# Four graph layers on TensorE: two more dense products in seven-product form, three norms' sums on ScalarE, and a plan with refined times

## The chip, the cores and the metric

The kernel runs on one core of a Trainium2 chip. The metric is the device time of one execution in microseconds (us). The core's engines are called by their short names: PE is TensorE (matmul), DVE is VectorE, ACT is ScalarE, POOL is GpSimd, SP is SyncE, which here only issues transfers.

## What is computed

A batch of 32 samples, each with 512 tokens of 256 features (x) and an own 512 x 512 weighted adjacency, goes through four layers in float32. Every layer adds its result to its input and normalizes each token over its 256 features:

```
x = layernorm(x + L0(x))   # agg = adj@x + (1+eps)*x;  relu(agg@W1 + b1) @ W2 + b2      256 -> 512 -> 256
x = layernorm(x + L1(x))   # h = adj @ (x@W.T + b);  where(h > 0, h, alpha*h)          256 -> 256
x = layernorm(x + L2(x))   # h = layernorm(x);  x + relu((adj@h)@W_rel + b_rel + h@W_root)
x = layernorm(x + L3(x))   # agg = adj@x + eps*x;  silu(rmsnorm(agg@W1 + b1)) @ W2 + b2 256 -> 1024 -> 256
```

`layernorm(v)` is `(v - mean) / sqrt(var + 1e-5)`, with mean and variance over the features of a token.

## The kernel before, in words

**Layout.** The 512 tokens lie on 128 partitions in four chunks (NC = 4), so x of one sample is a tile of 128 x 4 x 256, one "room" of SBUF. There are 38 rooms of 4 KB a partition, 12 small tiles ("few") of 64 numbers, and eight PSUM banks ("ps").

**Seven products.** A product of two 2 x 2 block matrices can be had from seven block products and some sums of blocks instead of eight block products (`seven`, line 554). The sums of the left factor come from `left_sums` (572) and, for weights, once for the whole run, from `weight_sums` (588); those of the right factor from `right_sums` (580), four subtractions per use. `seven` hands over each product as it is done: `take` and `put` add it from PSUM to the result, or copy it there. Three PSUM banks hold the running products. Before the change this form is used for the aggregation with the adjacency (`aggregate`, 649), for the first dense layers of layers 0 and 3 (`dense_feat`, 689) and for the second dense layer of layer 3 (written out inside `layer3`, lines 891 to 931, with 128-column matmuls).

**Eight products.** The second dense layer of layer 0, the dense layer of layer 1 and the two dense layers of layer 2 (W_root and W_rel, added up in one PSUM bank) use `dense_tok` (677). It takes one half of the tokens (two chunks) at a time and runs matmuls with 256 moving columns: four chunks of the contraction times two token chunks per half in layers 0 and 2.

**Norms.** `Norm` (740) is used by all four layers. `half` takes the statistics of two chunks on DVE, with `bn_stats` (128x256 to six numbers) and `bn_aggr` (to mean and variance). `scales` turns variances into `1/sqrt` with a POOL power. `scaled` applies scale and shift to each chunk, on ACT or DVE. Layer 1 takes two scalings from the same statistics, for its own norm and for the one that opens layer 2.

**The order.** Nothing is issued in program order. Every operation is first recorded in a `Plan` (178) with a cost for each engine that may run it (lines 35 to 68). `order` (303) then lists the operations: it keeps a clock per engine, picks the engine that can start first, and on it, among operations that could start within SOON, the one with the lowest rank. The rank is the sample's number times a period of 50 us plus the moment at which TensorE will need the result (`needs`, 273). Up to four samples are under way at a time (FLIGHT). Rooms, small tiles and banks are handed out in that order, with some kept back from later samples. YIELD makes an operation that could run on ACT or DVE prefer ACT. `best` (297) tries the RULES and keeps the order that its own clock likes most. What comes out is fixed in advance: each engine's queue runs strictly in that order, with semaphores between engines. All operations are issued from two places, so the profile shows them under line 248 (the order's `issue`) and tells them apart by tiles and shapes.

Of the kernel before, what the change touches and what calls it, by code (L numbers as in the profile page):

```python
# [2 lines left out]

# [10 lines left out]
P = 128  # L14
# [5 lines left out]
def span(ap):  # L20

    n = 1
    for d in ap.shape[1:]:
        n *= d
    return n
# [19 lines left out]


def stats_time(n):
    return 0.095 + n * 0.00092, 0.082


def scalar_time(n):
    return 0.19 + n * 0.00078, 0.1

# [19 lines left out]

SOON = 0.1


YIELD = 0.4

# [3 lines left out]

RULES = [(50, 2, last, 2) for last in (12, 20)]

# [93 lines left out]
class Plan:  # L178
# [52 lines left out]

    def do(self, out, *ways, ordered=None):

        ins = []
        port = set()
        for e, method, _, args, kw in ways:
            tiles = [x for x in (*args, *kw.values()) if isinstance(x, (bass.AP, Part))]
            ins += tiles
            if e == "gpsimd" and kw.get("op") != ALU.pow or e == "vector" and not (
                method.startswith("bn_") or any(in_psum(x) for x in tiles)  # L240
            ):
                port.add(e)

        def issue(engine, method, args, kw):
            def put(x):
                return x.place() if isinstance(x, Part) else x

            getattr(getattr(self.nc, engine), method)(  # L248
                put(out), *(put(x) for x in args), **{k: put(x) for k, x in kw.items()}
            )  # L250

        self.add(
            {
                e: (times, lambda e=e, m=method, args=args, kw=kw: issue(e, m, args, kw))
                for e, method, times, args, kw in ways
            },
            out, ins, ordered, port,
        )
# [127 lines left out]
def tile_gnn_stack(ctx: ExitStack, tc: tile.TileContext, a: dict, out: bass.AP):  # L386
# [35 lines left out]
    FH = FC3 // 2  # L422
    FLIGHT, ROOMS, SMALL = 4, 38, 12

# [21 lines left out]

    def scalar(func, n, x, **kw):
        return "scalar", "activation", scalar_time(n), (x,), dict(func=func, **kw)

# [8 lines left out]
    def act(o, x, func, **kw):  # L458
        plan.do(o, scalar(func, span(o), x, **kw))

    def copy(o, x):
# [18 lines left out]
    def stt(o, x, s, y, op0, op1):  # L480
        plan.do(o, vector("scalar_tensor_tensor", span(o), x, s, y, op0=op0, op1=op1))

# [66 lines left out]
    make_identity(nc, ident)  # L549
    mhalf = constant("mhalf", [P, 2 * NC])  # L550
    nc.vector.memset(mhalf, -0.5)

# [26 lines left out]

    def right_sums(b11, b12, b21, b22, t):  # L580

        sub(t[0], b12, b11)
        sub(t[1], b22, t[0])
        sub(t[2], b22, b12)
        sub(t[3], b21, t[1])
        return dict(m1=b11, m2=b21, m3=b22, m4=t[3], m5=t[0], m6=t[1], m7=t[2])

# [7 lines left out]
    def quarters(W):  # L595

        n = W.shape[-1] // 2
        return (W[:, k, i * n : (i + 1) * n] for i in range(2) for k in range(2))


    class Adjacency:
# [33 lines left out]
        def with_loops(self, loop):  # L635
            for d, o in zip(self.plain, self.loops):
                add(o, d, loop.unsqueeze(1).to_broadcast(list(o.shape)))

# [10 lines left out]
    def aggregate(x, adjacency):  # L649
# [5 lines left out]
        t = room(4, HC, P)  # L655
        right = right_sums(*blocks, [t[:, i] for i in range(4)])

# [31 lines left out]
    def dense_feat(aT, left, bias, hT, done):  # L689


        n = hT.n // 2
        t = room(4, TH)
        right = right_sums(
            *(aT[:, k, j * TH : (j + 1) * TH] for k in range(2) for j in range(2)),
            [t[:, i, :] for i in range(4)],
        )
        for f0 in range(0, n, 2):
# [22 lines left out]
            seven(*(bank(2, TH) for _ in range(3)), product, take, put)  # L721

    def column_sums(t, put):

# [15 lines left out]
    class Norm:  # L740


        def __init__(self, r):
            self.r = r
            few = small(64)
            cut = lambda at, n: few[:, at : at + n]
            self.st = [cut(6 * c, 6) for c in range(NC)]
            self.mv = cut(24, 2 * NC).then(lambda v: v.rearrange("p (c i) -> p c i", i=2))
            self.ve, self.rstd, self.shift = (cut(32 + 8 * i, 8) for i in range(3))

        def half(self, h):
            for c in range(h * HC, (h + 1) * HC):
                r = self.r[:, c, :]
                plan.do(self.st[c], ("vector", "bn_stats", stats_time(D), (r,), {}))
                plan.do(self.mv[:, c, :], ("vector", "bn_aggr", stats_time(6), (self.st[c],), {}))

        def scales(self, *affine):

            n = self.n = len(affine) * NC
            for i, (m, plus) in enumerate(affine):  # L760
                o = self.ve[:, i * NC : (i + 1) * NC]
                ts(o, self.mv[:, :, 1], m, plus, ALU.mult, ALU.add)
            inv_sqrt(self.rstd[:, 0:n], self.ve[:, 0:n])

        def scaled(self, i=0):

            y = self.r if (i + 1) * NC == self.n else tok()
            s, shift = (t[:, i * NC : (i + 1) * NC] for t in (self.rstd, self.shift))
            stt(shift, self.mv[:, :, 0], -1.0, s, ALU.mult, ALU.mult)
            for c in range(NC):  # L770
# [3 lines left out]
                    vector(  # L774
                        "tensor_scalar", D, r, self.mv[:, c, 0:1], scale,
                        op0=ALU.subtract, op1=ALU.mult,
                    ),
                    scalar(AF.Identity, D, r, scale=scale, bias=shift[:, c : c + 1]),
                )
            return y  # L780

    def plus_row(x, r):
# [21 lines left out]
    def layer0(x, adjacency):  # L804
# [7 lines left out]
        norm = Norm(x)  # L812
        for h in range(2):
            ps = dense_tok([(h1.chunk(k), W2_0[:, k, :]) for k in range(FC0)], h)
            add(half(x, h), ps, half(x, h))
            norm.half(h)
        norm.scales((1.0, LN_EPS))
# [28 lines left out]
    def layer2(h, xx, u, adjacency):  # L846
# [8 lines left out]
        norm = Norm(xx)  # L855
        for h in range(2):
            ps = dense_tok(
                [(hT.chunk(k), Wroot[:, k, :]) for k in range(DC)]
                + [(aT[:, k, :], Wrel[:, k, :]) for k in range(DC)], h,
            )  # L860
            add(half(u, h), ps, half(u, h))
            stt(half(xx, h), half(u, h), 0.0, half(xx, h), ALU.max, ALU.add)
            norm.half(h)
        adjacency.with_loops(loop3)
        norm.scales((1.0, LN_EPS))
        return norm.scaled()

    def layer3(x, adjacency, b):
# [20 lines left out]
        for c in range(NC):  # L889
            flip(pr[:, c * P : (c + 1) * P], rstd[:, c : c + 1].spread(P, P))  # L890
        t1, t2, t4 = (room(FH, TH) for _ in range(3))
        for q in range(0, FH, 2):
            for f in (q, q + 1, FH + q, FH + q + 1):
                mul(hT.chunk(f), hT.chunk(f), pr)
                act(hT.chunk(f), hT.chunk(f), AF.Silu, scale=w_3[:, f : f + 1])
            b11, b12 = (hT.pair(q)[:, :, j * TH : (j + 1) * TH] for j in range(2))
            b22 = hT.pair(FH + q)[:, :, TH:N]
            t1q, t2q = t1[:, q : q + 2], t2[:, q : q + 2]
            sub(t1q, b12, b11)
            sub(t2q, b22, t1q)  # L900
            sub(b12, b22, b12)
            sub(t4[:, q : q + 2], hT.pair(FH + q)[:, :, 0:TH], t2q)
        norm = Norm(x)

        def block(i, j):
            return x[:, j * HC : (j + 1) * HC, i * P : (i + 1) * P]

        def factor(m, k):
            if m in ("m4", "m5", "m6"):
                return dict(m4=t4, m5=t1, m6=t2)[m][:, k, :]  # L910
            f = k if m in ("m1", "m7") else FH + k
            j = 0 if m in ("m1", "m2") else 1
            return hT.chunk(f)[:, j * TH : (j + 1) * TH]

        def product(m, ps, first):
            for k in range(FH):
                for i in range(HC):
                    mm(
                        ps[:, i, :], factor(m, k)[:, i * P : (i + 1) * P], A2_3[m][:, k, :],
                        first and i == 0 and k == 0, k == FH - 1,  # L920
                    )

        def take(ps, i, j):
            add(block(i, j), ps, block(i, j))

        def put(ps, i, j, more):
            take(ps, i, j)
            if i == 1:
                norm.half(j)

        seven(*(bank(HC, P) for _ in range(3)), product, take, put)
        norm.scales((1.0, LN_EPS))
# [15 lines left out]
    b2_0 = row("L0_gnn_b2")  # L948
    W2_0 = weight("L0_gnn_W2")
    alpha = row("L1_gnn_alpha")  # L950
    nalpha = constant("nalpha", [P, 1])
# [10 lines left out]
    shift_2 = fold_norm(Wroot, "shift_2")  # L962
    add(shift_2, shift_2, b_2)
    h = layer1(x, adjacency)
    W1_3 = weight("L3_gnn_W1")
# [7 lines left out]
    A1_3 = weight_sums("A1_3", *quarters(W1_3))  # L973
    A2_3 = weight_sums(
        "A2_3",
        *(W2_3[:, k * FH : (k + 1) * FH, i * P : (i + 1) * P] for i in range(2) for k in range(2)),
    )
    layer3(layer2(*h, adjacency), adjacency, 0)
# [46 lines left out]
```

## Time and profile before

| | us |
|---|---|
| median of three runs | 2394.66 (2393.58 to 2394.78) |
| the profiled execution's own time | 2392.34 |
| its span, first to last instruction | 2390.6 |
| PE busy | 2361.3 |
| PE weight loads busy | 2113.1 |
| DVE busy | 2076.0 |
| ACT busy | 1195.2 |
| POOL busy | 391.1 |

A row of the profile names line, engine, operation, tiles written and read, shape and count; then the busy time of the group, the mean duration of one in nanoseconds, the engine's idle time just before them, and what ended that idle time. Tile names stand without numbers: `A` are sums of weights, `L_gnn_W` weights, `room`, `few` and `ps` as above. A float32 matmul leaves two records, each with a weight load of its own; a transposition by the identity (`ident`) leaves one. Durations in a group overlap where an engine is pipelined, so the busy time (a union) divided by the count can be below the mean. In the slices, each digit is the busy share of a fortieth of the span in tenths.

The largest waits that the trace shows are of engines that have little to do: POOL waited 1558.3 us for small DVE results, ACT 735.6 us for PE. DVE waited 202.7 us for PE and 42.6 for ACT. PE waited 10.3 us for the first x, 6.9 for DVE and 2.6 for ACT.

### The profile page before, as it was taken

What the parts mean: (1) busy time and instruction counts of PE and PEld (TensorE: products, weight loads), DVE (VectorE), ACT (ScalarE), POOL (GpSimd) and SP (SyncE); (2) the same over time, 40 slices, a digit from 0 to 9 for tenths busy, and PEclk for the clock granted to TensorE, in tenths of its full rate; (3) what the DMA queues carried; (4) which work ended last, traced back from release to release, by engine and by line L of the source; (5) the groups of instructions that cost most, each with busy time, mean ns of one, the idle gap of its engine ahead of it and who ended that gap; (6) DMA issues with size and microseconds to landing.
All of it is one profiled execution on the core that took longest, in us unless ns stands there. A gap on an engine that the chain in (4) does not pass through costs nothing.

```text
span 2390.6 us, 36106 instructions
## 1 busy us (share of the span) xinstructions
PE 2361.3 (99%) x12808; PEld 2113.1 (88%) x12808; DVE 2076.0 (87%) x5449; ACT 1195.2 (50%) x2417; POOL 391.1 (16%) x422
## 2 busy tenths in 40 slices
PE   7999999999999999999999999999999999999998
PEld 6889889988889888898888989888898888988887
DVE  6978988889888898888988888988889888888798
ACT  2445555455544455544555445554445554444564
POOL 1111111111112111211111111111111111111111
PEclk9999999999999999999999999999999999999999
DMA  7001013011111011110111101111101111010100
GB/s 229 14 1 33 30 54 95 18 39 53 54 51 43 14 53 54 51 49 9 52 53 54 49 23 37 53 54 49 47 12 53 54 49 55 12 54 1 54 1 36
DMA packets 104548, 107.47 MB, mean 45 GB/s; under 512 B 10928, under 2 KB 79280, under 8 KB 104368
## 3 DMA queue, kind: packets, MB, share of 16 engines
q1 hardware_dynamic: 100208, 104.62, 14.1%
q8 instruction: 101, 1.65, 0.3%
q10 hardware_dynamic: 4160, 0.54, 0.2%
q14 instruction: 79, 0.65, 0.1%
HBM read 54.80 MB, written 16.78 MB: 30 GB/s over the span
## 4 chain that ended last, share of the span: by engine, by line
PE 95%; DVE 3%; DMA 1%; ACT 1%; issue 0%; POOLq 0%; POOL 0%; ACTq 0%; SPq 0%; DVEq 0%
PE ps L248 95%; DVE room L248 2%; DVE few L248 1%; ACT room L248 1%; DMA room<-room 0%; DMA room<-in_adj_dram 0%; DMA L_gnn_ln_gamma_c<-in_L_gnn_ln_gamma_dram 0%; DMA L_gnn_b_c<-in_L_gnn_b_dram 0%; ACT L248 0%; POOLq L1021 0%; POOL few L248 0%; DVE L_gnn_W L248 0%; DVE A L248 0%; SPq L264 0%; ACTq L1021 0%
## 5 line engine op out<-in xcount | busy, mean ns | idle before, releaser
L248 PE MATMUL ps<-room,room 128*128 128x256 f32 x3584 | 951.8, 381 | 14.0 <-DMA room<-in_x_dram 10.3
L248 PEld LDWEIGHTS ps<-room,room 128*128 128x128 f32 x3584 | 646.7, 191 | 94.2 <-DMA room<-in_x_dram 10.3
L248 DVE TENSOR_TENSOR room<-ps,room 128x256 f32<-128x256 f32 (+1 forms) x1024 | 531.0, 526 | 212.7 <-PE ps L248 166.9
L248 PE MATMUL ps<-L_gnn_W,room 128*128 128x128 f32 (+1 forms) x3584 | 667.1, 320 | 2.6 <-ACT room L248 1.5
L248 PEld LDWEIGHTS ps<-L_gnn_W,room 128*128 128x128 f32 x3584 | 581.6, 191 | 61.1 <-ACT room L248 2.4
L248 DVE TENSOR_TENSOR room<-room,room 128x512 f32<-128x512 f32 (+1 forms) x928 | 500.5, 557 | 10.2 <-DMA room<-in_adj_dram 4.6
L248 ACT ACTIVATE room<-room,few 128x256 f32<-128x256 f32 x588 | 311.6, 592 | 328.5 <-DVE few L248 328.4
L248 ACT ACTIVATE room<-ps 128x256 f32<-128x256 f32 (+1 forms) x545 | 220.3, 407 | 498.5 <-PE ps L248 494.6
L248 POOL TENSOR_TENSOR few<-few,mhalf 128x4 f32<-128x4 f32 (+1 forms) x160 | 200.4, 1253 | 1558.5 <-DVE few L248 1558.3
L248 ACT ACTIVATE room<-ps,L_gnn_b_c 128x256 f32<-128x256 f32 x768 | 320.1, 470 | 246.1 <-PE ps L248 241.0
L248 PE MATMUL ps<-room,L_gnn_W 128*128 128x256 f32 x1536 | 439.5, 379 | 2.9 <-DVE room L248 2.8
L248 PE MATMUL ps<-room,A 128*128 128x256 f32 x1152 | 323.9, 379 | 0.2 <-ACT room L248 0.2
L248 PEld LDWEIGHTS ps<-room,L_gnn_W 128*128 128x128 f32 x1536 | 285.0, 190 | 40.0 <-DVE room L248 4.7
L248 DVE TENSOR_TENSOR room<-room 128x256 f32<-128x256 f32 (+1 forms) x576 | 266.8, 478 | 16.4 <-DMA room<-in_adj_dram 10.8
L248 POOL TENSOR_TENSOR room<-room,L_gnn_b 128x256 f32<-128x256 f32 x256 | 190.8, 753 | 434.9 <-PE ps L248 261.6
L248 ACT ACTIVATE room<-room 128x1024 f32<-128x1024 f32 (+1 forms) x256 | 238.2, 947 | 31.9 <-DVE room L248 31.2
L248 PEld LDWEIGHTS ps<-A,room 128*128 128x128 f32 x1536 | 226.9, 191 | 16.5
L248 PEld LDWEIGHTS ps<-room,A 128*128 128x128 f32 x1152 | 210.2, 190 | 27.1 <-ACT room L248 0.6
L248 PE MATMUL ps<-A,room 128*128 128x128 f32 x1536 | 233.4, 274 | 0.0
L248 DVE BATCH_NORM_STATS2 few<-room 128x6 f32<-128x256 f32 x512 | 203.9, 405 | 0.3
L248 ACT ACTIVATE room<-room,L_gnn_rms_weight_c 128x512 f32<-128x512 f32 x256 | 167.5, 712 | 73.0 <-DVE room L248 72.8
L248 DVE TENSOR_TENSOR room<-room,ps 128x512 f32<-128x512 f32 x256 | 161.9, 681 | 2.6 <-PE ps L248 2.5
(44 smaller groups left out, 1263.8 us busy)
## 6 DMA issues: line engine op xcount, KB each, us to landing
room<-in_adj_dram SPq DMA_DIRECT2D x128, 256.0 KB, 4.8
room<-room SPq DMA_DIRECT2D x256, 128.0 KB, 2.2
room<-in_x_dram SPq DMA_DIRECT2D x32, 512.0 KB, 5.9
out_dram<-room SPq DMA_DIRECT2D x32, 512.0 KB, 3.0
L_gnn_W<-in_L_gnn_W_dram SPq DMA_DIRECT2D x2, 1024.0 KB, 7.6
L_gnn_W<-in_L_gnn_W_dram SPq DMA_DIRECT2D x2, 512.0 KB, 5.3
L_gnn_b<-in_L_gnn_b_dram ACTq DMA_DIRECT2D x3, 128.0 KB, 4.2
L_gnn_W_rel<-in_L_gnn_W_rel_dram SPq DMA_DIRECT2D x1, 256.0 KB, 5.2
```

The lines of the kernel that those rows point to most:

```text
L248: getattr(getattr(self.nc, engine), method)(put(out), *(put(x) for x in args), **{k: put(x) for k, x in kw.items()})
```

## The change

There are four parts.

1. **Two more places in seven products.** `dense_sums` and `dense_add` are made out of what stood in `layer3`, and layers 0 and 2 use them in place of `dense_tok`. In layer 2, the transposed h and the aggregate are the two halves of one contraction of 512, W_root and W_rel the two halves of its weights, so that its two dense layers become one. With layer 0's second dense layer these are the "three more dense layers" of the change. `dense_tok` stays in layer 1. Two more sets of weight sums, A2_0 and A_2, are made once.
2. **Mean and variance of three norms on ACT.** The norms of layers 0, 1 and 2 take, per chunk, an Identity activation whose sum over the row is kept (`accum_out`), a DVE multiplication of two chunks' sums by -1/256, and a Square activation with that as its bias whose sum is kept. The element-wise results are not read; they go to two places, `scrap0` and `scrap1`, in turn. The norm of layer 3 keeps `bn_stats` and `bn_aggr` (`NormOnVector`).
3. **Fewer rooms.** 36 instead of 38. `right_sums` writes one of its four results over a block of its input. Layer 3's sums lie in six half-filled rooms where they lay in three full ones, layers 0 and 2 take three half-filled ones each.
4. **The plan's figures.** ACT's cost now depends on how many of scale and bias are columns; summing activations and DVE operations with a column have costs of their own. SOON goes from 0.1 to 0.06, YIELD from 0.4 to 0.8, and six RULES are tried instead of two. `with_loops` is named as vector work, as it was.

```diff
+def columns_time(n):
+    return 0.12 + n * 0.00106, 0.085
-def scalar_time(n):
-    return 0.19 + n * 0.00078, 0.1
+def scalar_time(n, columns):
+    return 0.035 + n * 0.00089 + columns * 0.113, 0.105
+def total_time(n, columns):
+    return 0.187 + n * 0.00089 + columns * 0.1, 0.1
-SOON = 0.1
-YIELD = 0.4
-RULES = [(50, 2, last, 2) for last in (12, 20)]
+SOON = 0.06
+YIELD = 0.8
+RULES = [(50, 2, last, near) for last in (12, 20) for near in (0, 0.5, 1)]
...
-    FLIGHT, ROOMS, SMALL = 4, 38, 12
+    FLIGHT, ROOMS, SMALL = 4, 36, 12
...
+    def total(o, x, func, **kw):
+        plan.do(o, scalar(func, span(x), x, times=total_time, **kw), scrap=next(scraps))
...
+    scraps = cycle([constant(f"scrap{i}", [P, D]) for i in range(2)])
...
+    def dense_sums(upper, lower):
+        right = {}
+        for pairs in zip(upper, lower):
+            blocks = [x[:, :, j * TH : (j + 1) * TH] for x in pairs for j in range(2)]
+            sums = right_sums(*blocks, [room(2, TH) for _ in range(3)], blocks[1])
+            for m, x in sums.items():
+                right.setdefault(m, []).extend(x[:, e, :] for e in range(2))
+        return right
+
+    def dense_add(x, right, left, done):
+        def block(i, j):
+            return x[:, j * HC : (j + 1) * HC, i * P : (i + 1) * P]
+        def product(m, ps, first):
+            n = len(right[m])
+            for k in range(n):
+                for i in range(HC):
+                    mm(
+                        ps[:, i, :], right[m][k][:, i * P : (i + 1) * P], left[m][:, k, :],
+                        first and i == 0 and k == 0, k == n - 1,
+                    )
+        def take(ps, i, j):
+            add(block(i, j), ps, block(i, j))
+        def put(ps, i, j, more):
+            take(ps, i, j)
+            if i == 1:
+                done(j)
+        seven(*(bank(HC, P) for _ in range(3)), product, take, put)
...
         def half(self, h):
-            for c in range(h * HC, (h + 1) * HC):
-                r = self.r[:, c, :]
-                plan.do(self.st[c], ("vector", "bn_stats", stats_time(D), (r,), {}))
-                plan.do(self.mv[:, c, :], ("vector", "bn_aggr", stats_time(6), (self.st[c],), {}))
+            chunks = range(h * HC, (h + 1) * HC)
+            for c in chunks:
+                total(self.first[:, c : c + 1], self.r[:, c, :], AF.Identity)
+            mine = slice(h * HC, (h + 1) * HC)
+            ts(self.less[:, mine], self.first[:, mine], -1.0 / D, None, ALU.mult)
+            for c in chunks:
+                total(
+                    self.second[:, c : c + 1], self.r[:, c, :], AF.Square,
+                    bias=self.less[:, c : c + 1],
+                )
...
-        for h in range(2):
-            ps = dense_tok([(h1.chunk(k), W2_0[:, k, :]) for k in range(FC0)], h)
-            add(half(x, h), ps, half(x, h))
-            norm.half(h)
+        dense_add(x, dense_sums(h1.rooms[:1], h1.rooms[1:]), A2_0, norm.half)
...
-        for h in range(2):
-            ps = dense_tok(
-                [(hT.chunk(k), Wroot[:, k, :]) for k in range(DC)]
-                + [(aT[:, k, :], Wrel[:, k, :]) for k in range(DC)], h,
-            )
-            add(half(u, h), ps, half(u, h))
+        def done(h):
             stt(half(xx, h), half(u, h), 0.0, half(xx, h), ALU.max, ALU.add)
             norm.half(h)
+        dense_add(u, dense_sums(hT.rooms, [aT]), A_2, done)
...
-        norm = Norm(x)
+        norm = NormOnVector(x)
+        dense_add(x, right, A2_3, norm.half)
...
+    A2_0 = weight_sums("A2_0", *blocks_of(W2_0[:, 0:2], W2_0[:, 2:]))
+    A_2 = weight_sums("A_2", *blocks_of(Wroot, Wrel))
```

## The prediction

> **What bounds the kernel now.** I read the page's busy table and slices first, to see whether one engine is full throughout.
>
> ```profile
> PE 2361.3 (99%) x12808; PEld 2113.1 (88%) x12808; DVE 2076.0 (87%) x5449; ACT 1195.2 (50%) x2417; POOL 391.1 (16%) x422
> PE   7999999999999999999999999999999999999998
> DVE  6978988889888898888988888988889888888798
> PEclk9999999999999999999999999999999999999999
> ```
>
> PE (TensorE matmul) is busy in all slices but the first and last, at full granted clock. DVE is second, ACT half empty. A busy PE is not yet a binding one, so the chain of waits in order of time comes next: is PE's stretch broken anywhere?
>
> ```profile
> by line: PE ps L248 94.5%; DVE room L248 2.1%; DVE few L248 0.8%; ACT room L248 0.7%; DMA room<-room 0.4%; issue 0.4%; DMA room<-in_adj_dram 0.2%; DMA L_gnn_ln_gamma_c<-in_L_gnn_ln_gamma_dram 0.2%; DMA L_gnn_b_c<-in_L_gnn_b_dram 0.2%; ACT L
> ...
> 315.74 1818.33 PE ps L248 x9853
> ```
>
> 1818 us on end the chain never leaves PE: the middle is paced by matmul issue. Idle PE is 2390.6 - 2361.3 = 29.3 us, 17 of it before 150 us, 2 around 2130 to 2180 us and 11 at the very end. So the sum is: change of PE work, plus change of PE's idle time.
>
> Rows' mean durations overlap (matmuls are pipelined), so the pitch is read from PE's timeline, start to next start:
>
> ```profile
> 425.97 1.89 PE L248 MATMUL ps<-L_gnn_W_root,room 128*128 128x256 f32 x8
> 427.70 0.60 PE L248 MATMUL ps<-ident,few 128*128 128x128 f32 x4
> ...
> 430.73 2.17 PE L248 MATMUL ps<-L_gnn_W,room 128*128 128x128 f32 x18
> 432.73 0.60 PE L248 MATMUL ps<-L_gnn_W_rel,room 128*128 128x256 f32 x2
> ```
>
> A float32 matmul leaves two records. 256 columns: (427.70 - 425.97) / 4 = 0.432 us. 128 columns: (432.73 - 430.73) / 9 = 0.222 us; I take 0.224, since ten such records from 2347.86 us on take 1.12 us to the next start.
>
> **PE's part.** dense_tok of layers 0 and 2 goes: 16 matmuls of 256 columns each, times 32 samples, 1024. dense_add replaces it: 7 products x 2 chunks x 2 row blocks = 28 of 128 columns, 56 per sample, 1792. The layer-3 product had this form already and keeps its 56. Sum: 1792 x 0.224 - 1024 x 0.432 = 401.4 - 442.4 = -41.0 us.
>
> One rule of the Trainium skill speaks against this: "TensorE: Matmul & The Clock Gate", section "Back-to-back issue gap", says that in a stream of load-then-multiply pairs the spacing is set by both, about 81 ns at 128 columns and 131 ns at 512, so that halving the columns saves much less than half. Interpolated to 98 ns at 256 (my estimate from that page), the 128-column matmul would cost 0.83 of 0.432, 0.357 us, and the change would add 1792 x 0.357 - 442.4 = +197 us. The row decides: 0.222 us in a run of nine, each with its own weights loaded. A float32 pass is long enough to cover its load. I take -41.0.
>
> **DVE's part.** Its rows:
>
> ```profile
> L248 DVE TENSOR_TENSOR room<-ps,room 128x256 f32<-128x256 f32 x608 | 248.3, 419 | 176.5 <-PE ps L248 140.8 <-ACT room L248 32.1
> L248 DVE TENSOR_TENSOR room<-room,room 128x512 f32<-128x512 f32 x480 | 321.0, 685 | 6.1 <-DMA room<-in_adj_dram 4.6 <-ACT room L248 0.5
> L248 DVE BATCH_NORM_STATS2 few<-room 128x6 f32<-128x256 f32 x512 | 203.9, 405 | 0.3
> L248 DVE BATCH_NORM_AGGREGATE few<-few 128x2 f32<-128x6 f32 x512 | 86.6, 171 | 2.7
> ```
>
> Busy time over count is each price: 0.408, 0.669, 0.398, 0.169. Removed: 384 statistics (-152.8) and 384 aggregates (-64.9), three norms of four; 128 PSUM adds of 512 elements at 0.682 (-87.3). Added: 448 PSUM adds of 256 elements, seven per layer (+182.8); 256 right-hand sums of 512 elements, four per layer (+171.3); 256 two-column negations, nearest the four-column scalar row at 0.147 (+37.6); 160 shifts change form, -160 x 0.268 + 160 x 0.195 (-11.7). Chunks that the planner moves between ACT and DVE, from the two instruction queues: 35 fewer normalizations, 22 more copies (-4.6). Eight weight sums once (+3.2). In all +74 us, to 2150, or 67.2 us a sample, where PE needs 2320 / 32 = 72.5.
>
> In the middle all of it lies beside PE work. Cover for it: 9.8 us of DVE idleness per sample now (2390.6 - 2076.0 over 32), of which 2.3 are filled and 1.3 vanish with PE's own shortening. How full may DVE be before PE stalls? Busy time by stretch answers:
>
> ```profile
> 350.00:1000.00 650.00, 650.00 (x3547) 583.26 (x3546) 570.91 (x1500) 329.51 (x669) 110.25 (x118) 1.00 0.15 48
> ...
> 2300.00:2360.00 60.00, 60.00 (x416) 56.49 (x415) 55.48 (x122) 32.21 (x59) 7.26 (x7) 1.00 0.00 1
> ```
>
> Columns after the length are PE, PEld, DVE, ACT, POOL. DVE at 87.8% over 650 us and at 92.5% over 60 us cost PE nothing; the fullest 50 us stretch (850 to 900) has 47.8 us, 95.6%, PE still whole. The new mean, 2150 / 2357 = 91%, lies inside what short stretches show and above what long ones do.
>
> **ACT's part.** 768 summing activations. No row shows an activation that accumulates. Nearest: 0.381 us without a column operand (`room<-ps`, 128x256), 0.417 with one, 0.530 with two. Below: 384 x (0.381 + 0.417) = 306 us. Above, with another half on top: 460. I take the plan's own figures in the code, 0.415 and 0.515: 357 us, ACT 1195 to about 1560, 66% busy. It is hidden either way; a gain is excluded, since they are new work on an engine that must run them.
>
> Latency is another matter. A half's mean was statistics and aggregates, about 1.1 us on DVE. Now: two sums, a DVE negation, two squares, 0.83 + 0.15 + 1.03 = 2.0 us, with two more hand-overs. About +1.2 us per norm. The squares wait for the negation, and behind them on ACT stand the bias activations that empty PSUM; behind the negation, which waits for ACT, stand PSUM adds on DVE. PE waits for both through its banks. In the middle other samples' work fills this. 365 of the 768 sums also wait for ACT's own earlier write to the same place, as the plan's order breaks the alternation: between 0 and 0.2 us each, at most 73 us on an engine with 800 idle.
>
> **Idle PE at both ends.** Start: eight more weight sums and layer 0's first right-hand sums fall where the chain already runs on DVE (35 to 44, 55 to 64, 85 to 92 us): 0 to 6 us, I take +3. End: the last sample has few others beside it; three norms at +1.2 us and its share of extra DVE work, in a stretch where the chain is on DVE anyway (2335 to 2365): 0 to 6, I take +3. The last norm stays on DVE, so the 11 us after the last matmul stay, plus 0.15 for the negation. Better planning figures may take back up to 4 us of the 17 at the start (a quarter, my judgement). No DMA is added or moved between queues; two rooms fewer (36) and six half-filled ones for three full ones in layer 3 are priced among the rivals.
>
> **Sum.** Span 2390.6 - 41.0 + 6 = 2355.6. The profiled execution took 2392.34, 1.7 above its span, and the median is 2394.66, 2.3 above that. The same distances give 2355.6 + 4.1 = 2359.7, so 2360.
>
> **Rivals.**
> The bare PE sum: both ends stay, or better figures win back 4 us: 2394.66 - 41.0 = 2353.7, or 2350. For it: the middle's unbroken 1818 us. Against: both ends already run on DVE.
> Local stalls: seven PE-to-DVE hand-overs per layer where there were two, three PSUM banks held for 6.3 us, 36 rooms. At 0.5 us a sample, 2360 + 16 = 2376. For it: DVE's long-run share goes where no 650 us stretch has been. Against: PE waited for DVE only 6.9 us, and DVE waits 202.7 us for PE, which is slack.
> Slower: DVE becomes the bound. Its 2150 us take 2391 at a share of 89.9%; that is the deciding point. If the in-order queues can't hold more than the 88% of the long stretches, the span is 2150 / 0.88 = 2443, the time 2447. Against: 92.5% and 95.6% above, without a stall.
> No gain: 128-column matmuls in long unmixed runs are paced by the weight loads and eat the 41 us: 2395. It needs 0.023 us on each of 1792. The same page's section on loading weights gives columns / 1.2, an estimate of 107 ns per pass, just under the 112 ns pitch seen: for it, the thin margin; against, the run of nine, which shows no stretch.
>
> **Chances.** Forecast (2354 to 2368) 0.62; bare sum 0.14; local stalls 0.16; slower 0.05; no gain 0.03. A measurement of this kernel can tell about 0.2%, 5 us, from no change. So faster 0.92, same 0.03, slower 0.05. The range, 2349 to 2379, leaves out the last two and the worse end of the stalls.
>
> **What would show it.** Right: PE busy near 2320 with the same two pitches; DVE near 2150; chain on PE through the middle; idle PE 30 to 40 us, all at the ends. Wrong: gaps on PE in the middle released by DVE (stalls, or DVE as the bound, with DVE above 95%), by ACT (the sums' latency), or a 128-column pitch well above 0.224 us.

## The result, and the profile after

The changed kernel takes 2368.02 us (median of four runs, 2366.55 to 2370.03), the kernel before 2394.72 in the same session. The ratio is 0.9887 [0.987, 0.9905]: 1.1% faster, inside the range on record and 8 us above the forecast. The profiled execution took 2368.86 us with a span of 2366.9.

The page's busy table and slices of the changed kernel:

```profile
PE 2326.3 (98%) x14344; PEld 2135.9 (90%) x14344; DVE 2138.2 (90%) x5508; ACT 1564.5 (66%) x3966; POOL 404.7 (17%) x422
PE   7999999999999999999999999999999999999997
DVE  6899999999899999899999999999999999988997
PEclk9999999999999999999999999999999999999999
```

Against before: PE busy fell by 35.0 us, 41.0 were forecast; DVE rose by 62 (74 forecast); ACT is where it was expected. The idle time of PE, span less busy, rose from 29.3 to 40.6 us, where 35 were forecast. The two misses, 6.0 and 5.3 us, are the whole 11.3 us by which the span is above 2355.6. Only 8 remain in the median, since it lies 1.1 us above this span, where the forecast had put 4.1 between the two.

The chain of waits, in order of time, shows where:

```profile
by line: PE ps L264 93.3%; DVE room L264 2.8%; ACT scrap L264 0.7%; issue 0.6%; DVE few L264 0.5%; ACT room L264 0.5%; DMA room<-in_x_dram 0.3%; DMA L_gnn_ln_gamma_c<-in_L_gnn_ln_gamma_dram 0.2%; SPq L278 0.2%; DMA room<-room 0.2%; DMA L_gn
...
61.68 2.57 DVE room L264 x6
64.27 1.32 DVE room L264 x3
65.66 2.20 DVE room L264 x4
68.95 1.01 ACT scrap L264 x4
71.22 0.98 ACT scrap L264 x4
...
160.22 1896.25 PE ps L264 x11774
...
2110.38 3.94 DVE room L264 x9
2114.77 4.43 DVE room L264 x9
```

For 1896 us the chain never leaves PE: the middle is as unbroken as before. Before and behind it the chain runs over DVE's sums and adds (`room`) and the new summing activations (`scrap`).

A busy PE can hide short gaps, since matmuls are pipelined. So I split every span from the starts of PE's records: each record at its own pitch (0.112 us at 128 columns, 0.216 at 256) is "work", and what the steps between starts have beyond that is "lost". With the time to the first matmul (10.0 to 11.6 us everywhere) and from the last one on (8.3 to 9.5) it makes the span. A middle slightly below zero says that the pitch is rounded up a little (two 128-column records in a row are 111.4 ns apart on the mean in the changed kernel's middle). Start and end are the 200 us after the first matmul and all from 2000 us after it. In some spells the trace grants PE a clock of 0.50; the last column says how much of start and end that is, counting the pitch of every record started in them a second time.

| kernel | median us, ratio [95%] | span | work | lost: start | middle | end | half clock, start / end |
|---|---|---|---|---|---|---|---|
| before | 2394.72 | 2390.6 | 2353.7 | 11.7 | 0.7 | 4.6 | 0 / 0 |
| after | 2368.02, 0.9887 [0.987, 0.9905] | 2366.9 | 2312.8 | 24.0 | -3.3 | 14.5 | 3.4 / 1.8 |
| figures_alone | 2389.28, 0.9969 [0.9958, 0.9981] | 2388.0 | 2353.7 | 10.9 | -0.8 | 4.1 | 0 / 0 |
| sums_alone | 2395.07, 0.9998 [0.9989, 1.0006] | 2396.4 | 2353.7 | 12.2 | -1.3 | 11.6 | 1.9 / 1.8 |
| norms_dve | 2477.24, 1.0343 [1.0327, 1.0359] | 2475.5 | 2312.8 | 27.2 | 84.3 | 31.4 | 4.6 / 4.7 |
| old_figures | 2414.86, 1.0078 [1.0066, 1.0091] | 2413.1 | 2312.8 | 23.3 | 38.0 | 19.8 | 3.1 / 3.5 |
| old_costs | 2397.09, 1.0005 [0.9997, 1.0014] | 2394.4 | 2312.8 | 23.6 | 20.2 | 18.2 | 1.8 / 1.8 |
| old_search | 2394.6, 0.9997 [0.9989, 1.0005] | 2397.3 | 2312.8 | 24.1 | 18.2 | 22.7 | 3.4 / 5.6 |
| old_soon_yield | 2379.11, 0.9932 [0.992, 0.9945] | 2378.9 | 2312.8 | 25.0 | 3.3 | 18.6 | 1.8 / 3.3 |
| ends_0_4 | 2370.95, 0.9895 [0.9881, 0.9908] | 2370.9 | 2312.8 | 20.8 | -3.3 | 20.3 | 0 / 5.9 |
| scrap1 | 2376.59, 0.9919 [0.9905, 0.9932] | 2375.8 | 2312.8 | 24.8 | 1.7 | 16.9 | 1.6 / 1.8 |
| rooms34 | 2383.16, 0.9948 [0.9935, 0.996] | 2382.7 | 2312.8 | 26.8 | -3.1 | 26.7 | 1.7 / 3.6 |
| eight_2_4 | 2359.28, 0.9849 [0.9836, 0.9862] | 2356.1 | 2320.5 | 13.1 | -2.8 | 6.1 | 0 / 0 |
| eight_last16 | 2355.46, 0.9833 [0.9819, 0.9846] | 2353.0 | 2320.5 | 12.3 | -2.8 | 2.6 | 0 / 0 |

Ratios are against the kernel before on the same chip. The spans and what stands behind them are of one execution each; those of sums_alone and old_search took 3.1 and 4.5 us more than their medians. So the change did to the span: work -40.9, middle -4.0, start +12.3, end +9.9, time ahead of the first and behind the last matmul -1.0; together -23.7. Of the -4.0, some 2 us are the rounding of the pitch (3584 more records at 0.6 ns). Of the +22.2 at the ends, 5.2 are half clock. The forecast had +6 for both ends.

Two stretches at the start make it plain; the columns are PE, PEld, DVE, ACT and POOL busy, granted clock, DMA share and GB/s:

```profile
20.00:60.00 40.00, 35.61 (x181) 30.75 (x180) 30.36 (x82) 15.91 (x43) 5.32 (x7) 0.96 0.66 217
60.00:100.00 40.00, 34.86 (x207) 30.70 (x206) 35.43 (x93) 25.52 (x78) 5.33 (x6) 0.96 0.05 14
350.00:1000.00 650.00, 650.00 (x4040) 599.19 (x4039) 596.20 (x1542) 442.12 (x1118) 113.61 (x117) 1.00 0.15 45
```

In the first two PE misses 4 to 5 us each, and the clock was not whole. In the third PE issues 4040 records where it issued 3547 before; at 448 and 400 a sample (14344 and 12808 over 32) that is 72.1 us a sample instead of 73.3, some 39 us over 32 samples. DVE is at 91.7% there without costing PE anything.

### The profile page after: what moved, and what is told of

Its sections match the earlier page's. It is cut to its first block, busy times and chain, and to the rows that moved or that the text cites. A ratio compares the mean times of both kernels' runs of the same rounds, so it can differ in the third digit from the quotient of the medians.

```text
span 2366.9 us, 41198 instructions
## 1 busy us (share of the span) xinstructions
PE 2326.3 (98%) x14344; PEld 2135.9 (90%) x14344; DVE 2138.2 (90%) x5508; ACT 1564.5 (66%) x3966; POOL 404.7 (17%) x422
## 4 chain that ended last, share of the span: by engine, by line
PE 93%; DVE 3%; ACT 1%; DMA 1%; issue 1%; SPq 0%; POOL 0%; POOLq 0%; ACTq 0%; DVEq 0%
PE ps L264 93%; DVE room L264 3%; ACT scrap L264 1%; DVE few L264 1%; ACT room L264 0%; DMA room<-in_x_dram 0%; DMA L_gnn_ln_gamma_c<-in_L_gnn_ln_gamma_dram 0%; SPq L278 0%; DMA room<-room 0%; DMA L_gnn_b_c<-in_L_gnn_b_dram 0%; POOL few L264 0%; POOLq L1064 0%; DVE A L264 0%; ACTq L1064 0%; ACTq L278 0%
## 5 line engine op out<-in xcount | busy, mean ns | idle before, releaser
L264 PE MATMUL ps<-room,room 128*128 128x256 f32 x3584 | 922.5, 382 | 18.7 <-DMA room<-in_x_dram 12.6
L264 DVE TENSOR_TENSOR room<-ps,room 128x256 f32<-128x256 f32 (+1 forms) x1344 | 633.5, 479 | 139.8 <-PE ps L264 114.9
L264 DVE TENSOR_TENSOR room<-room,room 128x512 f32<-128x512 f32 (+1 forms) x1120 | 638.0, 582 | 8.3 <-DMA room<-in_adj_dram 3.3
L264 PE MATMUL ps<-L_gnn_W,room 128*128 128x128 f32 (+1 forms) x3584 | 628.7, 292 | 5.3 <-ACT room L264 3.9
L264 PEld LDWEIGHTS ps<-L_gnn_W,room 128*128 128x128 f32 x3584 | 537.5, 193 | 34.9 <-ACT room L264 5.1
L264 PE MATMUL ps<-A,room 128*128 128x128 f32 x3072 | 480.2, 276 | 2.7 <-ACT room L264 2.6
L264 PEld LDWEIGHTS ps<-A,room 128*128 128x128 f32 x3072 | 426.8, 193 | 13.6 <-ACT room L264 2.8
L264 DVE TENSOR_TENSOR room<-room 128x256 f32<-128x256 f32 (+1 forms) x640 | 324.5, 511 | 12.2 <-DMA room<-in_adj_dram 4.1
L264 ACT ACTIVATE scrap<-room,few 128x256 f32<-128x256 f32 x384 | 191.2, 499 | 67.0 <-DVE few L264 66.9
L264 ACT ACTIVATE scrap<-room 128x256 f32<-128x256 f32 x384 | 157.8, 411 | 37.6 <-DVE room L264 30.3
```

The costliest lines, as they stand in the source:

```text
L264: getattr(getattr(self.nc, engine), method)(to, *(put(x) for x in args), **kw)
```

## The experiments

The theories of the expectations: A, the seven products give the gain and their DVE work and hand-overs cost the ends; B, ScalarE's longer way to mean and variance costs the ends; C, DVE can be filled to 98%; D, the gain is the plan's; E, it is the cost functions that carry the plan; F, it is the search (SOON, YIELD, RULES); G, within it the nearness in RULES; H, SOON and YIELD. Every run but scrap1 gets a new order from the planner, and one order was measured for each setting: a difference of a few us holds the luck of that order too.

**One part alone.** sums_alone keeps ScalarE's sums and the new figures, with eight products in layers 0 and 2:

```diff
-        dense_add(x, dense_sums(h1.rooms[:1], h1.rooms[1:]), A2_0, norm.half)
+        for h in range(2):
+            ps = dense_tok([(h1.chunk(k), W2_0[:, k, :]) for k in range(FC0)], h)
+            add(half(x, h), ps, half(x, h))
+            norm.half(h)
```

and the same in layer 2, without the two sets of weight sums.

> The change with layers 0 and 2 back in eight products (256 columns); the three norms' sums stay on ScalarE, the plan keeps its new figures and 36 rooms. Theory A (the 41 us of TensorE work come from the seven products alone, and the 11 us lost against the forecast at both ends come from the extra VectorE work and the hand-overs of the seven products): TensorE busy back at 2361, VectorE down to about 1860, idle TensorE at the ends as before or a little less, time 2388 to 2396. Rival B (the ends lose because the sums on ScalarE lengthen each norm): the ends lose 10 us here too, time 2400 to 2408.

It took 2395.07 us, no change from before. Its middle stretch:

```profile
350.00:1000.00 650.00, 650.00 (x3553) 584.27 (x3552) 524.86 (x1356) 427.00 (x1100) 108.40 (x117) 1.00 0.14 43
```

DVE has come down to 80.7% and PE issues as many records as before (3553 against 3547): an emptier DVE is worth nothing where PE is the bound. Without the seven products, then, the sums and the figures together leave the time where it was.

norms_dve keeps the seven products and the figures and puts statistics back on DVE:

```diff
-        norm = Norm(x)
+        norm = NormOnVector(x)
```

in all layers.

> The change with all four norms on VectorE (bn_stats, bn_aggr); seven products in layers 0 and 2 stay. TensorE work as in the change (2320 us), VectorE work 2138 + 384 x 0.567 - 43 = about 2310. Theory A (VectorE becomes the bound when its work nears TensorE's; the sums on ScalarE are what lets the seven products pay): TensorE gets gaps in the middle released by VectorE, time 2420 to 2490, slower than before. Rival C (VectorE can be filled to 98% as TensorE can): 2370 to 2390.

2477.24 us, 3.4% slower than before. The page's busy table, its middle stretch and two of its waits (sum us, how many, longest):

```profile
PE 2369.5 (96%) x14344; PEld 2139.6 (86%) x14344; DVE 2262.8 (91%) x6221; ACT 1238.8 (50%) x2485; POOL 404.6 (16%) x422
```

```profile
350.00:1000.00 650.00, 630.76 (x3873) 571.26 (x3872) 604.99 (x1664) 332.06 (x665) 107.11 (x108) 1.00 0.14 44
```

```profile
PEld ps L264 <- DVE room L264: 74.6, 75, 5.0
...
PE ps L264 <- DVE room L264: 51.9, 52, 4.8
```

DVE is at 93.1% in the middle, and PE waits for it all along. So DVE holds PE up, well short of theory C's 98%: the rival of the prediction that ends on the slow side, met when the sums are left where they were.

figures_alone is the kernel before with the changed cost functions, SOON, YIELD and RULES:

```diff
...
-def scalar_time(n):
-    return 0.19 + n * 0.00078, 0.1
+def scalar_time(n, columns):
+    return 0.035 + n * 0.00089 + columns * 0.113, 0.105
...
-SOON = 0.1
-YIELD = 0.4
-RULES = [(50, 2, last, 2) for last in (12, 20)]
+SOON = 0.06
+YIELD = 0.8
+RULES = [(50, 2, last, near) for last in (12, 20) for near in (0, 0.5, 1)]
```

> The kernel before with the plan's new figures only (costs by columns, SOON 0.06, YIELD 0.8, six rules). Same work on each engine. Theory A: the middle is paced by matmul issue and can't change; only the ends can, by a few us: 2386 to 2396. Rival D (a good part of the gain is the plan's): below 2380.

2389.28 us, 0.3% or 7 us below the kernel before of its session. With eight products the figures are worth little. The parts in a row: figures -7, sums on top +6 (with the 36 rooms, which sums_alone keeps too), seven products on top of both -27; without the sums the seven products cost +88.

**The figures, with seven products in place.** old_figures is the changed kernel with the old cost functions, SOON, YIELD and RULES (the last diff backwards, `total_time` as the old `scalar_time`, `columns_time` as `vector_time`).

> The change with the plan's figures of before (one cost for ScalarE, also for its sums, SOON 0.1, YIELD 0.4, two rules). Theory A: the middle stays on TensorE, the ends differ by a few us: 2364 to 2376. Rival D (the refined figures carry part of the gain, since VectorE is fuller now and a wrong order costs more): 2380 or more.

It took 2414.86 us: slower than before, and 47 above the changed kernel. Its middle stretch and three waits:

```profile
350.00:1000.00 650.00, 640.15 (x3965) 582.22 (x3965) 611.76 (x1518) 416.12 (x1068) 106.71 (x113) 1.00 0.14 42
```

```profile
PEld ps L264 <- ACT room L264: 41.0, 77, 2.1
...
PEld ps L264 <- DVE room L264: 37.2, 46, 3.1
...
DVE few L264 <- ACT scrap L264: 23.4, 51, 1.7
```

The same waits of the changed kernel:

```profile
DVE few L264 <- ACT scrap L264: 15.7, 36, 1.0
...
PEld ps L264 <- ACT room L264: 13.5, 16, 2.8
PEld ps L264 <- DVE room L264: 12.7, 13, 3.5
```

The operations are nearly the same, only their order and the choice between ACT and DVE differ, and DVE even looks fuller (94.1%). PE's weight loads wait 41.0 us for ACT instead of 13.5 and 37.2 for DVE instead of 12.7.

Which of the figures? old_costs has only the old cost functions, old_search only the old SOON, YIELD and RULES.

> The change with only the plan's cost functions of before (ScalarE 0.19 + 0.00078 n whatever its columns, also for its sums; VectorE operations with a column as others); SOON, YIELD and the six rules stay new. The run with all old figures took 2414.9, with gaps in the middle. Theory E (the costs carry it: the plan believes that a sum with a column takes 0.39 where the trace shows about 0.5 to 0.6, so it queues VectorE and TensorE work behind ScalarE results that come late): gaps in every period of the middle, 2395 to 2420. Rival F (the search carries it): 2364 to 2376.

> The change with only the search figures of before (SOON 0.1, YIELD 0.4, two rules); the cost functions stay refined. Theory E (the costs carry it): 2366 to 2380. Rival F (the search carries it: with VectorE over 90% full it must get work sooner off it, and nearness weighed with 2 delays what TensorE needs): 2395 to 2420.

2397.09 and 2394.6 us: each half by itself costs the whole gain, 29 and 27 us. E and F are both half right, and with both halves old the loss is 47, not 56. old_soon_yield has the old SOON and YIELD with the new RULES:

```diff
-SOON = 0.06
-YIELD = 0.8
+SOON = 0.1
+YIELD = 0.4
```

> The change with SOON 0.1 and YIELD 0.4 of before; costs and the six rules stay new. With all three search figures of before it took 2394.6. Theory G (the rules' nearness of 2 is what hurts, as it puts TensorE's inputs behind other work): 2366 to 2376. Rival H (YIELD and SOON hurt, as they leave more chunks on the full VectorE): 2385 to 2396.

2379.11 us, +11, between the ranges of G and H. So of old_search's 27 us, the rest, some 16, goes with the rules (nearness 2 instead of 0, 0.5 and 1, and two orders to choose from instead of six); that is a difference of two runs, not a run of its own, and the nearness was not parted from the number of orders.

The middle of old_costs teaches something about reading. Its stretch and, of the whole run, its largest wait on PE's side:

```profile
350.00:1000.00 650.00, 649.84 (x3997) 588.73 (x3996) 593.14 (x1516) 436.47 (x1112) 111.79 (x115) 1.00 0.15 45
```

```profile
PEld ps L264 <- ACT room L264: 43.4, 156, 2.8
```

PE shows 649.84 of 650 us busy, and yet issued 3997 records where the changed kernel issued 4040, 1.1% fewer. The 156 small waits of the weight loads must lie where matmuls already under way still count as busy. Records per time show such gaps (20.2 us lost in the table's middle), the busy share doesn't.

**The ends.** eight_2_4 takes eight products in layers 0 and 2 for the first two samples and the last four, seven for the 26 between. The weight sums, which overwrite a block of the weights, are made when sample 2 begins and taken back before the last four:

```diff
-        dense_add(x, dense_sums(h1.rooms[:1], h1.rooms[1:]), A2_0, norm.half)
+        if 2 <= plan.graph < B - 4:
+            dense_add(x, dense_sums(h1.rooms[:1], h1.rooms[1:]), A2_0, norm.half)
+        else:
+            for h in range(2):
+                ps = dense_tok([(h1.chunk(k), W2_0[:, k, :]) for k in range(FC0)], h)
...
+        if b == 2:
+            A2_0 = weight_sums("A2_0", *blocks_of(W2_0[:, 0:2], W2_0[:, 2:]))
...
+        if b == B - 4:
+            for left in (A2_0, A_2):
+                sub(left["m5"], left["m5"], left["m4"])
```

> The change, but the first two samples and the last four run layers 0 and 2 in eight products (the sums of those weights are made when the third sample starts and taken back, m5 - m4, when the last four start). It adds 6 x 1.28 = 7.7 us of TensorE work. Theory A (the seven products cost at both ends, where few other samples cover their VectorE work and hand-overs): idle TensorE at the ends falls by 12 to 18 us, time 2358 to 2364, faster than the change. Rival B (the ScalarE sums of the norms cost at the ends): the 7.7 us are paid and nothing comes back, 2372 to 2378.

2359.28 us, 9 below the changed kernel. In the spans: work +7.7 (six samples with more of it), start -10.9, end -8.4, middle and the rest +0.8. Of the 19.3 us that came back at the ends, 5.2 are half clock that is gone; the other 14.1 lie within the 12 to 18 expected. The run takes the hand-overs, the right-hand sums and the 3.2 us of weight sums from the start together, so it does not tell them apart; of weight sums, the chain of the changed kernel holds less than 1 us there. The stretch from 60 us on and the one from 2000 us on, first of eight_2_4:

```profile
60.00:100.00 40.00, 38.44 (x181) 33.18 (x180) 35.79 (x95) 27.54 (x84) 8.31 (x7) 1.00 0.05 14
...
2000.00:2200.00 200.00, 199.40 (x1073) 178.50 (x1072) 161.43 (x425) 128.53 (x341) 34.84 (x37) 1.00 0.16 49
```

and of the changed kernel, where the first was shown above:

```profile
2000.00:2200.00 200.00, 196.26 (x1184) 178.09 (x1184) 178.55 (x457) 129.80 (x343) 33.33 (x35) 1.00 0.16 48
```

At the end DVE has 17 us less to do in 200, ACT as much as it had, and PE's gaps shrink from 3.7 to 0.6 us. At the start the clock stays whole.

Theory B's own test gives the norms of the last four samples back to DVE and keeps their seven products:

```diff
-        norm = Norm(x)
+        norm = (NormOnVector if plan.graph < 0 or plan.graph >= B - 4 else Norm)(x)
```

in layers 0, 1 and 2.

> The change, but the norms of the last four samples take mean and variance on VectorE again. Rival B (the latency of the ScalarE sums costs at the end): 5 to 8 us faster than the change, 2360 to 2363. Theory A (VectorE work and hand-overs cost there): no faster, 2366 to 2378, since four samples get 6.8 us of VectorE work each back in a stretch where VectorE is full.

2370.95 us, nothing gained. The end lost 20.3 instead of 14.5, but two spells of 6.8 us at half clock, from 2113 and 2345 us on, are 5.9 of that; without the clock it is 14.4 against 12.7. B as the main cause of the end falls. It isn't free of blame: sums_alone lost 11.6 at the end (9.8 without the clock) where figures_alone lost 4.1. But eight_2_4, with the same sums and eight products in its last four samples too, lost 6.1. The order that the planner happens on has a share of some us in that region, and I can't divide it further.

rooms34 takes two more rooms away (`ROOMS` 34 instead of 36).

> The change with 34 rooms instead of 36. If rooms limit how far the samples overlap where VectorE is full, it loses at both ends and perhaps in the middle: 2376 to 2395. If the 36 rooms are enough and two fewer change nothing: 2366 to 2372.

2383.16 us, +15, with start and end at 26.8 and 26.7 and a whole middle (4039 records in its 650 us). Half clock is 5.3 of the 53.5, about what the changed kernel had. Rooms limit the ends and not the middle. Whether the change's own step from 38 to 36 cost anything wasn't tried; sums_alone, with 36 rooms and eight products, lost 12.2 at the start, 10.3 without the clock, where the kernel before lost 11.7.

**The two places.** scrap1 has all unread elements written to one place:

```diff
-    scraps = cycle([constant(f"scrap{i}", [P, D]) for i in range(2)])
+    scraps = cycle([constant(f"scrap{i}", [P, D]) for i in range(1)])
```

> The change with one place for the unread elements of the sums instead of two in turn; the order of all instructions stays. 523 of the 768 sums then wait for ScalarE's own earlier write (365 with two places). Theory A (ScalarE has 800 us idle and hides it): 2366 to 2371, ScalarE waits a little longer. Rival (the norms' chain is on the path, each wait of 0.1 to 0.2 us delays VectorE and TensorE behind it): 2375 to 2395.

2376.59 us, +8.6. I had thought it hidden. Its middle stretch and two waits:

```profile
350.00:1000.00 650.00, 650.00 (x4031) 592.49 (x4030) 594.69 (x1539) 448.35 (x1115) 113.58 (x117) 1.00 0.14 45
```

```profile
DVE few L264 <- ACT scrap L264: 35.5, 88, 1.2
...
PEld ps L264 <- ACT room L264: 30.7, 93, 3.1
```

Of the 768 sums 523 now wait for ACT's own earlier write (365 before). DVE waits longer for the sums (35.5 us against 15.7), ACT's evacuations of PSUM come later, and PE's weight loads wait 30.7 us for them against 13.5. The middle lost 5.0 us, start and end 3.2.

**A version that beats both.** eight_last16 is eight_2_4 with nine rules for the planner to try instead of six, `for last in (12, 16, 20)`.

> The run with eight products in the first two and last four samples (2359.3), with a third choice, 16, for the distance of the last samples in the rules. If what is left at the end is the plan's choice of order there: 2352 to 2358. If not: 2358 to 2361.

2355.46 us, ratio 0.9833 [0.9819, 0.9846]: 12.6 below the changed kernel. The end loses 2.6 us, less than before the change.

## Why the prediction was right or wrong

**PE's part: right.** The records at their pitch make -40.9 us against -41.0, but that is the forecast's own product of counts and pitches. What tests it is that the pitch held. Nine 128-column matmuls in the timeline of PE take what they took before:

```profile
87.88 2.17 PE L264 MATMUL ps<-A,room 128*128 128x128 f32 x18
89.89 0.39 PE L264 MATMUL ps<-L_gnn_W,room 128*128 128x128 f32 x2
```

(89.89 - 87.88) / 9 = 0.223 us. With all 3584 new 128-column records in, the middle had nothing lost. So the rule of the Trainium skill ("TensorE: Matmul & The Clock Gate", section "Back-to-back issue gap") from which the prediction had estimated +197 us doesn't hold for these float32 matmuls, and the rival "no gain" is out.

**The ends: the failed step.** "I take +3" at the start and "+3" at the end: they cost +12.3 and +9.9, both outside the bounds of 0 to 6. The prediction counted eight weight sums, layer 0's first right-hand sums, the longer norms and a share of DVE's extra work. The seven hand-overs per layer, in samples with few others beside them, stood only among its rivals, and the clock nowhere. Half clock is 3.4 and 1.8 us of the two (last section). With eight products at the ends, 7.5 and 6.6 of the remaining 8.9 and 8.1 us come back (eight_2_4): the seven products with all that they bring cost the larger part. That within them it is the hand-overs is argued from the chain over DVE, not shown by a run. The figures did not take back "up to 4 us of the 17 at the start": with eight products they took 0.8.

That the total came out near is luck in part. Of the 16.2 us missed at the ends, 4.0 came back in the middle, 1.0 outside the matmuls, and 3.0 because the median lies nearer to the span of the profiled execution than before; none of these was in the sum.

**DVE's part: the counts right, the prices too high, 12 us in all.** These rows of the changed kernel answer to those of before, of which the prediction did not show the last one here (L248):

```profile
L264 DVE TENSOR_TENSOR room<-room,room 128x512 f32<-128x512 f32 x672 | 461.0, 688 | 5.2 <-DMA room<-in_adj_dram 3.3 <-ACT room L264 0.2
L264 DVE TENSOR_TENSOR room<-ps,room 128x256 f32<-128x256 f32 x1056 | 437.7, 422 | 94.1 <-PE ps L264 71.4 <-ACT room L264 10.1
...
L264 DVE TENSOR_TENSOR room<-room 128x512 f32<-128x512 f32 x192 | 130.8, 682 | 5.0 <-DMA room<-in_adj_dram 4.1 <-ACT room L264 0.4
...
L264 DVE BATCH_NORM_STATS2 few<-room 128x6 f32<-128x256 f32 x128 | 53.9, 421 | 1.0
```

```profile
L248 DVE TENSOR_TENSOR room<-room 128x512 f32<-128x512 f32 x128 | 88.3, 690 | 12.8 <-DMA room<-in_adj_dram 10.8 <-ACT room L248 1.5
```

448 more PSUM adds, +189.4 us (+182.8 forecast); 256 more right-hand sums, 192 of them in the first row and 64 in `room<-room`, +182.5 (+171.3); 384 fewer statistics, -150.0 (-152.8). By the rows, then, the forecast was too low, and yet DVE rose by 12 us less. The rows overlap: all of them in that view add up to 2466 us where DVE was busy 2138.2, and before to 2355 where it was busy 2076.0. The prediction took a row's busy time over its count as the price and added the prices up. Counting each instruction only up to the start of DVE's next one, the PSUM adds make +155.8, the right-hand sums +154.5, statistics and aggregates -173.9, the wider PSUM adds -75.7, negations +27.2, the shifts -19.0 and all else -6.7, which is the 62.

**"In the middle all of it lies beside PE work": right for this order only.** The prediction took 88 to 95% of DVE as harmless from short stretches of before, whatever the order. It isn't: at 91.7% the changed kernel lost nothing, but old_costs at 91.3% lost 20 us of middle, old_search at 92.8% 18, old_figures at 94.1% 38, norms_dve at 93.1% 84; and old_soon_yield, at 93.9% (610.25 of 650), lost 3. A busy share doesn't tell whether an in-order queue holds; the rivals "local stalls" and "DVE becomes the bound" were real, and it took the new figures to keep them away. Here the prediction mis-sized a part by a factor: it gave the planning figures at most 4 us, at the start alone. With seven products in place they carry 47, 41 of them in the middle. This left the forecast near because it took an order that loses nothing for granted, and the order found is such a one; the shares that it read could not tell it so.

**ACT's part: right.** A summing activation turned out to be two instructions. ACT's timeline of the changed kernel, start and length:

```profile
619.01 0.42 ACT L264 ACTIVATE scrap<-room 128x256 f32<-128x256 f32 x1
619.33 0.19 ACT L264 ACTIVATION_READ_ACCUMULATOR scrap<-room 128x1 f32 x1
619.42 0.40 ACT L264 ACTIVATE scrap<-room 128x256 f32<-128x256 f32 x1
...
626.30 0.50 ACT L264 ACTIVATE scrap<-room,few 128x256 f32<-128x256 f32 x1
626.70 0.20 ACT L264 ACTIVATION_READ_ACCUMULATOR scrap<-room,few 128x1 f32 x1
626.79 0.50 ACT L264 ACTIVATE scrap<-room,few 128x256 f32<-128x256 f32 x1
```

The second one starts before the activation's end and is overlapped by the next: from start to start a sum takes 0.41 us, with a column bias 0.49, as taken (0.415 and 0.515). To the end of its read it is 0.51 and 0.60, which adds to a half's way to its variance: with DVE's negation (169 ns on the mean), 0.41 + 0.51 + 0.17 + 0.49 + 0.60 = 2.2 us, where 2.0 were forecast and 1.1 was the estimate for DVE. That ACT's 66% hides all of it was too simple, though. "Between 0 and 0.2 us each, at most 73 us on an engine with 800 idle" let the waits for ACT's own write count for nothing; scrap1, with 158 more of them in the same order, cost 8.6 us, some 0.05 us for each. What the 365 that the change has anyway cost was not tried.

## What to carry to other kernels

A form that trades matmul work for sums and hand-overs pays only where other work covers them; let the first and last units of a pipeline, which stand alone, keep the direct form (here 9 us, 13 with a better order; some 5 of them by keeping PE's clock whole). Where two in-order engines are above 90%, the cost figures and rules that fix the order are part of the change: tried by themselves they were worth 7 us here, under the heavier load 47. And to see whether the bounding engine really loses nothing, count its instructions per time in a steady stretch, since its busy share can stay at 100% while it slows by 1%.

## What the runs showed of the hardware that wasn't expected

**Half clock after the start.** The timeline of PE in the changed kernel holds stretches at twice the pitch:

```profile
36.87 1.97 PE L264 MATMUL ps<-room,room 128*128 128x256 f32 x4 [2.60 <-DMA room<-in_x_dram]
38.62 1.90 PE L264 MATMUL ps<-L_gnn_W,room 128*128 128x128 f32 x8
...
73.19 0.49 PE L264 MATMUL ps<-A,room 128*128 128x128 f32 x2 [2.62 <-ACT room L264]
...
76.04 0.64 PE L264 MATMUL ps<-L_gnn_W,room 128*128 128x128 f32 x2
76.46 0.64 PE L264 MATMUL ps<-A,room 128*128 128x128 f32 x2
```

(38.62 - 36.87) / 2 = 0.875 us for a 256-column matmul, 0.42 for a 128-column one. The granted clock around them, third column from the end:

```profile
36.00:41.00 5.00, 4.13 (x18) 3.81 (x19) 0.93 (x3) 0.00 (x0) 0.00 (x0) 0.66 0.96 292
72.00:78.00 6.00, 4.80 (x28) 4.81 (x29) 4.54 (x15) 3.71 (x8) 1.64 (x1) 0.72 0.00 0
```

At a clock of 0.50, 0.34 x 5 / 0.5 and 0.28 x 6 / 0.5 are 3.4 us each: from 36.95 and from 74.50 us on by the trace's record of the clock, and once more from 2344.4. Each costs some 1.7 us. The first follows a gap of 2.60 us at once, the second comes 1.3 us after the end of a gap of 2.62. The kernel before and both eight_ kernels had none after 25 us, though eight_2_4 had a gap as long:

```profile
43.90 2.19 PE L264 MATMUL ps<-room,room 128*128 128x256 f32 x8 [2.61 <-ACT room L264]
```

What the 14 traces agree on is where the gap lies. Between the first matmuls and the last they hold 29 spells at half clock; each lasts 3.41 us or twice that, and within a trace all of them begin on one grid of steps of 3.41 us. So I added up, for every step of the grid, the time in which PE had no record at its pitch. All 26 steps at full clock that were idle for more than 62% were followed by a spell (the three of the changed kernel were at 81, 65 and 62.3%); of six between 60 and 62%, three were; of some 9600 below, none. eight_2_4's gap lay across a border of the grid, and the step that held most of it was idle for 53%. Executions of one kernel differ accordingly: those of sums_alone took 2393.0 to 2395.3 us at a mean clock of 0.999 and 2396.8 to 2398.5 at 0.998 and 0.997. All this is read off traces; no run moved a gap on purpose.

**The read of the accumulator** is an instruction of its own, 187 to 189 ns on the mean, 768 times, but costs ACT no time where another activation follows.
